# Attention scores as two products in 64x128 tiles a step, in place of four in 64x64 tiles

## The chip, the core and the metric

The kernel runs on one core of a Trainium2 chip. The metric is the device time of one execution in microseconds (us). The kernel before took 1121.53 us, the median of three runs (1121.16 to 1121.66).

## The reference

All values are 32-bit floats. The input `x` has 8 batches of 512 rows of 256 columns. Four blocks follow one another, each with a layernorm in front and its result added to `x`: a linear attention without scores, a feed-forward block, a softmax attention with 16 heads of 64 columns, and the same feed-forward block again. The change is in the third block:

```python
q = jnp.einsum('bsd,hpd->bhsp', x, q_w) + q_b
k = jnp.einsum('bsd,hpd->bhsp', x, k_w) + k_b
v = jnp.einsum('bsd,hpd->bhsp', x, v_w) + v_b
scores = jnp.einsum('bhqp,bhkp->bhqk', q, k) / jnp.sqrt(jnp.float32(P))
attn = jax.nn.softmax(scores, axis=2)          # over the queries
ctx = jnp.einsum('bhqk,bhkp->bqhp', attn, v)
concat = ctx.reshape(ctx.shape[0], ctx.shape[1], H * P)
out = concat @ l_w.T + l_b
```

The softmax runs over the queries, so that each key has a maximum and a sum of its own. The kernel therefore keeps keys on partitions and queries along the row, and it divides the rows of `v`, not the scores, by the sums.

## The kernel before

**Heads go in pairs.** Eight batches of eight pairs make 64 pairs, numbered `g`. A pair's transposed queries and keys lie in one buffer `qk`: partitions 0 to 63 hold the first head's 64 columns, partitions 64 to 127 the second's. A pair has four steps `c`, one for each block of 128 keys. In the notes below a step is one pair and one block of keys.

**A step of scores** (`scores`, line 1308) takes a pair of PSUM banks, `ps[0]` for the first head and `ps[1]` for the second; there are three such pairs of banks, taken in turn. Each bank gets 128 keys by 512 queries. TensorE fills them with four products (line 1320): two halves of 64 keys by two heads. Each has 64 contraction rows (a head's columns) and 64 weight columns (half of the keys), and so takes a quarter of the 128x128 array. The four use the four quarters. VectorE then takes the negated maximum of each row into `nm` (line 1326). `exps` (line 1331) has ScalarE write `e`, the exponentials, with their row sums (line 1337), which frees the banks.

**A step of contexts** (`context`, line 1361) multiplies `e` by the scaled values `vs` (line 1374). It too has four products in 64x64 tiles: two halves of the keys are now the contraction rows, and two heads of 64 columns are the weight columns. The two halves go to two further banks, `cx[0]` and `cx[1]`, and add up there over the four steps of a pair. At the end ScalarE copies one bank (line 1381) and VectorE adds the other (line 1382). `scale_v` (line 1345) makes `vs` on GpSimd from the sums' reciprocals.

**The order within attention** is written out in `attend` (line 1387). Attention runs in stages of two pairs, or of four pairs once in each batch. In a stage's first pair each step of scores is followed by a step of contexts of the pair before. In the other pairs the contexts lag one step and the last two stand together. TensorE's order for a stage of two pairs, with s for a step of scores and c for a step of contexts, is

```
s c s c s c s c | s s c s c s c c
```

and each further pair of a four-pair stage repeats the right half. Nothing else of TensorE stands between the steps of a stage, except in the first two pairs, whose contexts do not follow the pattern yet.

**Between the stages** TensorE does everything else in products of the whole 128x128 array: projections of queries, keys and values for the pairs to come (lines 999 and 1036), the output projection (line 1186), the linear attention (line 728 and others) and the two feed-forward blocks. A planner (`Order`) writes the order down when the program is built: chains of steps with estimated costs and due times are interleaved by the engines' estimated free times. It charges a step of scores and a step of contexts 0.86 us of TensorE each, and it charges 0.1 us (`CHANGE`, line 30) at either end of a stage. All of it is fixed before the program runs; at run time each engine works its own list in order and waits on semaphores.

**Two passes for one product.** A product of 32-bit floats appears in the profile as two weight loads and two matmuls, one after the other. The 2048 matmuls of line 1320 are thus 1024 products: 64 pairs, four steps, four products.

Of the kernel before, what the change touches and what calls it, by code (L numbers as in the profile page):

```python
# [14 lines left out]
P = 128  # L15
B, S, D = 8, 512, 256
H, HD = 16, 64
# [260 lines left out]
def kernel(ctx: ExitStack, tc: tile.TileContext, a: dict, out: bass.AP):  # L278
# [13 lines left out]
    nc = tc.nc  # L292
# [71 lines left out]
    def psum_tile(i, name):  # L364
        return psum.tile([P, 512], F32, tag=f"ps{i}", name=name)
# [942 lines left out]
    def scores(g, c):  # L1308

        qt, kt = qk[g][:, 0, :], qk[g][:, 1, :]  # L1310
        h = c // 2
        if c % 2 == 0:
            sums[g, h] = small.tile([P, 2, 2], F32, tag="sums", name=f"sums_{g}_{h}")
        i, since = order.take_pair()
        ps = [psum_tile(2 * i + j, f"sc_{g}_{c}_{j}") for j in range(2)]
        for m in range(2):
            keys = slice(c * P + m * HD, c * P + (m + 1) * HD)
            for j in range(2):
                hs = slice(j * HD, (j + 1) * HD)
                nc.tensor.matmul(  # L1320
                    ps[j][m * HD : (m + 1) * HD, :], lhsT=kt[hs, keys], rhs=qt[hs, :],
                    start=True, stop=True,
                )
        nm = small.tile([P, 2], F32, tag="nm", name=f"nm_{g}_{c}")
        for j in range(2):
            nc.vector.tensor_reduce(nm[:, j : j + 1], ps[j], AX.X, ALU.max, negate=True)  # L1326
        ready = order.place("T", 0.86, max(since, order.marks[f"qk_{g - g % 2}"]))
        scored[g, c] = i, ps, nm, order.place("V", 1.2, ready)
        order.keep_pair(i, 1e9)
# [57 lines left out]
    def attend(first, n):  # L1387

        for g in range(first, first + n):
            behind = 1 if g > first else 0  # L1390
            for c in range(NT):
                if c == 3 and g < first + n - 1:
                    order.at_once(scale_v(g, 0))
                scores(g, c)
                if c == 1 and g > first:
                    order.at_once(scale_v(g - 1, 1))
                if g > 0 and c >= behind:
                    context(g - 1, c - behind)
                elif g == 0:
                    order.fill(BANK)  # L1400
                if behind and c == 3:
                    context(g - 1, 3)
                exps(g, c)
                order.fill(0.0, 1.0)
# [116 lines left out]
```

## Time and profile before

| | value |
| --- | --- |
| time, median of 3 runs | 1121.53 us |
| time of the profiled execution | 1121.81 us |
| its span, first to last instruction | 1119.7 us |
| TensorE matmuls (PE) | 1105.3 us busy, 99%, 6938 instructions |
| TensorE weight loads (PEld) | 743.6 us busy, 66%, 6938 instructions |
| VectorE (DVE) | 798.4 us, 71% |
| ScalarE (ACT) | 678.3 us, 61% |
| GpSimd (POOL) | 590.0 us, 53% |
| DMA engines, mean | 31 GB/s |
| granted TensorE clock | 1.000 |

The profile is of one execution, and its times are in microseconds from the start of the span. The time of the profiled execution is 2.1 us longer than the span. A row of a group names line, engine, operation, what is written and read, and the shape; then the number of instructions, the time in which at least one of them ran, the mean of one in nanoseconds, and the idle time of the engine before them. `64*64` or `128*128` ahead of a matmul's shape are the rows and columns of the array that it uses. Matmuls are pipelined and overlap, so that the distance between two starts says more than the duration of one. In a timeline the columns are start, length and the merged instructions of one group.

### The profile page before, as it was taken

Reading aid. Unit: us, or ns where it says so; the run is one execution under the profiler, and the core shown is the slowest. Engines: PE = TensorE matmul, PEld = TensorE weight load, DVE = VectorE, ACT = ScalarE, POOL = GpSimd, SP = SyncE. Lnnn points to the kernel's source line nnn. Section 1 sums busy time; section 2 is a strip of 40 time slices with the busy share of each in tenths; the row PEclk is TensorE's granted clock in tenths of the full one; section 3 lists DMA queues with packets and bytes.
Section 4 is the critical chain, followed back from the end, with each engine's and each line's share of the span. In section 5 each row is a group of like instructions: output and inputs, shape, how many; then the busy total and the mean of one; then the engine's idle time right before and its main releaser. Section 6 shows DMA issues by size and latency. Waiting matters only on the chain.

```text
span 1119.7 us, 19677 instructions
## 1 busy us (share of the span) xinstructions
PE 1105.3 (99%) x6938; PEld 743.6 (66%) x6938; DVE 798.4 (71%) x1749; ACT 678.3 (61%) x1779; POOL 590.0 (53%) x909
## 2 busy tenths in 40 slices
PE   7999999999999999999999999999999999999998
PEld 4655646676766777667767667677675766756557
DVE  5778587768677685776857687667786668766765
ACT  4665586359456584566836767556676467554663
POOL 3596425462565735757356563575644865254321
PEclk9999999999999999999999999999999999999999
DMA  8001001120112201111011120211101121001101
GB/s 296 15 11 30 10 2 20 20 39 1 20 38 39 39 1 21 53 22 38 11 29 38 20 38 2 57 20 20 38 11 29 20 39 20 1 20 34 19 2 38
DMA packets 83874, 34.18 MB, mean 31 GB/s; under 512 B 73152, under 2 KB 82496, under 8 KB 83264
## 3 DMA queue, kind: packets, MB, share of 16 engines
q1 hardware_dynamic: 82736, 31.74, 12.6%
q8 instruction: 55, 0.90, 0.3%
q10 hardware_dynamic: 1008, 1.18, 0.3%
q14 instruction: 43, 0.35, 0.1%
q0 software_dynamic: 32, 0.00, 0.0%
HBM read 10.89 MB, written 4.19 MB: 13 GB/s over the span
## 4 chain that ended last, share of the span: by engine, by line
PE 96%; DVE 2%; ACT 0%; issue 0%; POOL 0%; DMA 0%; DVEq 0%; ACTq 0%
PE sc L1320 20%; PE cx L1374 20%; PE m_qk L999 17%; PE m_v L1036 8%; PE m_y L1186 8%; PE kv L728 5%; PE o_g L473 2%; PE r_g L473 2%; PE o_f L473 2%; PE q L473 2%; PE k_f L585 2%; PE r_f L473 2%; PE m_k_g L646 2%; PE y L473 1%; PE v L1075 1%; PE qk L1292 1%
## 5 line engine op out<-in xcount | busy, mean ns | idle before, releaser
L1337 ACT ACTIVATE e<-sc,nm 128x512 f32<-128x512 f32 x512 | 346.2, 693 | 99.8 <-DVE nm L1326 98.4
L1326 DVE TENSOR_REDUCE nm<-sc 128x1 f32<-128x512 f32 x512 | 321.6, 681 | 21.9 <-PE sc L1320 20.6
L1320 PE MATMUL sc<-qk 64*64 64x512 f32 x2048 | 284.7, 593 | 0.2
L1374 PE MATMUL cx<-e,vs 64*64 64x512 f32 x2048 | 283.5, 590 | 0.0
L1354 POOL TENSOR_TENSOR vs<-v,rs 128x256 f32<-128x256 f32 x128 | 78.5, 614 | 256.9 <-DVE rs L1350 247.8
L1374 PEld LDWEIGHTS cx<-e,vs 64*64 64x64 f32 x2048 | 107.5, 133 | 115.8 <-issue 77.5
L1320 PEld LDWEIGHTS sc<-qk 64*64 64x64 f32 x2048 | 105.9, 132 | 112.8 <-issue 67.4
L1337 ACT ACTIVATION_READ_ACCUMULATOR e<-sc,nm 128x1 f32 x512 | 107.2, 209 | 0.0
L1007 ACT ACTIVATE qk<-m_qk,bias 128x256 f32<-128x256 f32 x124 | 52.0, 473 | 64.8 <-PE m_qk L999 64.3
L1382 DVE TENSOR_TENSOR ctx<-cx,ctx 128x512 f32<-128x512 f32 x64 | 44.3, 692 | 44.2 <-ACT ctx L1381 44.2
L1015 DVE SCALAR_TENSOR_TENSOR qk<-m_qk,dbias,qk 128x256 f32<-128x256 f32 x124 | 53.9, 478 | 21.3 <-PE m_qk L999 20.4
L1381 ACT COPY ctx<-cx 128x512 f32<-128x512 f32 x64 | 37.8, 590 | 33.5 <-PE cx L1374 33.0
L728 PE MATMUL kv<-wkv,xrFalse 128*128 128x512 f32 x112 | 53.6, 606 | 0.0
L452 POOL COPY xrFalse<-xnFalse 128x512 uint16<-128x512 uint16 x72 | 42.1, 616 | 4.8 <-ACT xnFalse L425 4.8
L461 POOL COPY xrFalse<-xkFalse 128x1024 uint16<-128x1024 uint16 x24 | 32.1, 1338 | 21.3 <-DMA xkFalse<-xrFalse 21.2
L1186 PE MATMUL m_y<-ctx,al 128*128 128x256 f32 x168 | 40.1, 381 | 0.0
L999 PE MATMUL m_qk<-xta,aq 128*128 128x256 f32 x124 | 37.4, 383 | 0.0
L999 PE MATMUL m_qk<-xta,sums_q 128*128 128x256 f32 x124 | 37.2, 382 | 0.0
L999 PE MATMUL m_qk<-xts,aq 128*128 128x256 f32 x124 | 37.0, 380 | 0.1
L999 PE MATMUL m_qk<-xts,ak 128*128 128x256 f32 x124 | 36.9, 379 | 0.0
L999 PE MATMUL m_qk<-xta,sums_k 128*128 128x256 f32 x124 | 36.9, 379 | 0.0
L999 PE MATMUL m_qk<-xta,ak 128*128 128x256 f32 x124 | 36.9, 379 | 0.0
(281 smaller groups left out, 2123.9 us busy)
## 6 DMA issues: line engine op xcount, KB each, us to landing
out<-x SPq DMA_DIRECT2D x15, 256.0 KB, 2.1
x<-in_x SPq DMA_DIRECT2D x6, 512.0 KB, 4.0
aq<-in_aq SPq DMA_DIRECT2D x1, 1024.0 KB, 8.2
ak<-in_ak SPq DMA_DIRECT2D x1, 1024.0 KB, 10.2
av<-in_av SPq DMA_DIRECT2D x1, 1024.0 KB, 12.2
al<-in_al SPq DMA_DIRECT2D x1, 1024.0 KB, 5.2
xkFalse<-xrFalse SPq DMA_TRANSPOSE x36, 3.0
x<-in_x ACTq DMA_DIRECT2D x4, 128.0 KB, 4.0
```

What stands on the lines that cost most here:

```text
L473: nc.tensor.matmul(ps[:, u * D : (u + 1) * D], lhsT=lhs[i][:, u * P : (u + 1) * P], rhs=rhs[i], start=(i == 0), stop=(i == n - 1),)
L728: nc.tensor.matmul(ps, lhsT=xt[:, kc, u * P : (u + 1) * P], rhs=wkv[:, kc, :], start=(kc == 0), stop=(kc == KC - 1),)
L999: nc.tensor.matmul(ps[:, w * HS : (w + 1) * HS], lhsT=lhs[w][n - 1], rhs=block_of_rows(b, n), start=start and w == 0, stop=True, skip_grou ...
L1007: nc.scalar.activation(dst[:, w, :], ps[:, w, :], AF.Identity, bias=bias[:, w, p : p + 1])
L1015: nc.vector.scalar_tensor_tensor(dst[:, w, :], ps[:, w, :], dbias[:, w, p // 2 : p // 2 + 1], part[:, w, :], ALU.add, ALU.add,)
L1036: nc.tensor.matmul(ps[:, u * HS : (u + 1) * HS], lhsT=block_of_rows(b, n)[:, u * P : (u + 1) * P], rhs=rhs[n - 1], start=start and u == 0, ...
L1186: nc.tensor.matmul(ps, lhsT=lhs[n - 1][:, g, :], rhs=rhs[g][n - 1], start=first and g == 0, stop=True, skip_group_check=True,)
L1320: nc.tensor.matmul(ps[j][m * HD : (m + 1) * HD, :], lhsT=kt[hs, keys], rhs=qt[hs, :], start=True, stop=True,)
L1326: nc.vector.tensor_reduce(nm[:, j : j + 1], ps[j], AX.X, ALU.max, negate=True)
L1337: nc.scalar.activation(e[:, j, :], ps[j], AF.Exp, bias=nm[:, j : j + 1], accum_out=sums[g, h][:, c % 2, j : j + 1],)
L1354: nc.gpsimd.tensor_tensor(vs, vh[b, p // 4][:, 2 * h : 2 * h + 2, cols].rearrange("p t (j d) -> p t j d", j=2), rs.unsqueeze(3).to_broadca ...
L1374: nc.tensor.matmul(cx[m][j * HD : (j + 1) * HD, :], lhsT=vsc[g, c // 2][ks, c % 2, j, :], rhs=es[g, c][ks, j, :], start=(c == 0), stop=(c ...
```

## The change

One product now covers all 128 keys of a block, so that a step of scores has two products in place of four, one for each head. Each has 64 contraction rows and 128 weight columns: half of the array's rows and all of its columns. Both write a bank of their own, as before. Contexts stay in 64x64 tiles. The maxima, the exponentials and the planner's estimates are not touched.

```diff
         ps = [psum_tile(2 * i + j, f"sc_{g}_{c}_{j}") for j in range(2)]
-        for m in range(2):
-            keys = slice(c * P + m * HD, c * P + (m + 1) * HD)
-            for j in range(2):
-                hs = slice(j * HD, (j + 1) * HD)
-                nc.tensor.matmul(
-                    ps[j][m * HD : (m + 1) * HD, :], lhsT=kt[hs, keys], rhs=qt[hs, :],
-                    start=True, stop=True,
-                )
+        for j in range(2):
+            hs = slice(j * HD, (j + 1) * HD)
+            nc.tensor.matmul(
+                ps[j], lhsT=kt[hs, c * P : (c + 1) * P], rhs=qt[hs, :], start=True, stop=True
+            )
         nm = small.tile([P, 2], F32, tag="nm", name=f"nm_{g}_{c}")
```

## The prediction

> **What bounds the kernel now.** I read the page first: engines, granted clock, chain of waits, costliest groups. The chain that ended last is TensorE for 96% of the span, and the two attention groups hold the most of it.
>
> ```profile
> PE 1105.3 (99%) x6938; PEld 743.6 (66%) x6938; DVE 798.4 (71%) x1749; ACT 678.3 (61%) x1779; POOL 590.0 (53%) x909
> ...
> PEclk9999999999999999999999999999999999999999
> ...
> PE 96%; DVE 2%; ACT 0%; issue 0%; POOL 0%; DMA 0%; DVEq 0%; ACTq 0%
> ...
> L1337 ACT ACTIVATE e<-sc,nm 128x512 f32<-128x512 f32 x512 | 346.2, 693 | 99.8 <-DVE nm L1326 98.4
> ...
> L1320 PE MATMUL sc<-qk 64*64 64x512 f32 x2048 | 284.7, 593 | 0.2
> L1374 PE MATMUL cx<-e,vs 64*64 64x512 f32 x2048 | 283.5, 590 | 0.0
> ...
> L1337 ACT ACTIVATION_READ_ACCUMULATOR e<-sc,nm 128x1 f32 x512 | 107.2, 209 | 0.0
> ```
>
> TensorE is never short of work and its clock is full, so whatever it gains or loses goes straight into the time. Next I read TensorE's timeline through one stage of two pairs, with the work on either side of it.
>
> ```profile
> 621.17 1.03 PE L1036 MATMUL m_v<-sums_v,xta 128*128 128x256 f32 x4
> 622.12 1.09 PE L1320 MATMUL sc<-qk 64*64 64x512 f32 x8
> 623.03 1.04 PE L1374 MATMUL cx<-e,vs 64*64 64x512 f32 x8
> 623.89 1.04 PE L1320 MATMUL sc<-qk 64*64 64x512 f32 x8
> ...
> 634.19 1.90 PE L1374 MATMUL cx<-e,vs 64*64 64x512 f32 x16
> 636.02 3.72 PE L585 MATMUL k_f<-xkFalse,fk 128*128 128x256 f32 x16
> 639.58 1.24 PE L473 MATMUL r_f<-fr,xrFalse 128*128 128x256 f32 x5
> ```
>
> Inside the stage a step of scores or contexts starts 0.86 us after the one before (623.03 to 623.89): eight passes in four tiles, so two rounds of 0.429. A pass of 256 columns in the whole array takes half of that, 0.2156. So the pace is the number of streamed columns, whatever the tile, and the four tiles of a round run side by side: single starts lie 7 ns apart.
>
> The changes of tile are dearer. **Into 64x64:** four passes from 621.17 end their turn at 622.03, but the scores start at 622.12, 0.09 late; and their first step lasts 0.91, not 0.86, another 0.05. **Out to 128x128:** two steps from 634.19 end their turn at 635.91, the fourth tile's 0.02 later, and the next product starts at 636.02, 0.09 late; its 16 passes take 3.56 in place of 3.45, another 0.105. Start by start, all 26 changes in and all 26 out agree: 0.093 to 0.095, then 0.051; 0.090 or 0.091, then 0.105.
>
> The weight loads' timeline, at the stage that begins at 583.48, tells the two parts apart.
>
> ```profile
> 582.74 0.41 PEld L473 LDWEIGHTS o_g<-fv,xnTrue 128*128 128x128 f32 x2
> 583.48 0.21 PEld L1320 LDWEIGHTS sc<-qk 64*64 64x64 f32 x8 [0.33 <-issue]
> 583.96 0.15 PEld L1374 LDWEIGHTS cx<-e,vs 64*64 64x64 f32 x4 [0.28 <-issue]
> 584.39 0.15 PEld L1374 LDWEIGHTS cx<-e,vs 64*64 64x64 f32 x4 [0.28 <-issue]
> ```
>
> Within one kind of tile the loads run a round ahead of their matmuls: loads for the contexts start at 583.96, the contexts at 584.39. At the change the first load starts only as the first matmul does, 583.48. So about 0.09 us is an emptying of the array, and the 0.05 (64 columns) or 0.105 (128 columns) behind it is a load that nothing hides.
>
> **The change part by part.** *Removed:* 512 products, so 1024 of 6938 matmuls and as many loads. This saves no stream time. A step is still two rounds of 512 columns, 2 x 0.429, because the four quarter tiles were already side by side, and the two halves will be if the two heads' row halves still overlap. Nothing in the trace shows 64x128; the bounds are 0.86 a step (halves overlap, as the two row halves of the 64x64 round do) and 1.72 (they don't). I take 0.86, which is the row with the same two row halves. Issue does not limit a pass (7 ns between starts), so fewer passes give nothing back.
>
> *Added:* changes of tile shape inside the stages. In the instruction order of the changed kernel TensorE's list is otherwise the same; it holds 212 places where contexts follow scores, 188 where scores follow contexts, and 25 entries from whole-array work into scores. Today all these steps are 64x64, and the first two kinds cost nothing.
>
> The price of a change between 64x64 and 64x128 is not in the trace. Below it is zero (a stop of the array can't win time of itself); the nearest rows are the 52 changes above, and I take them: the array empties (0.09), then loads for as many columns as the new tile has. Contexts after scores: 212 x (0.094 + 0.051) = 30.7 us. Scores after contexts: 188 x (0.090 + 0.105) = 36.7 us. Entries: the first load is 128 wide, not 64, 25 x 0.054 = 1.4 us. Together 68.8 us.
>
> The load of a 64x128 tile has half the rows of the 128x128 one; were it priced as a 64-column load, the sum falls by 188 x 0.054 = 10 us. Did the array empty twice as fast because only 64 rows are in use, it falls by 400 x 0.046 = 18 us.
>
> The Trainium skill (TensorEngine Tiling, Key Properties) says that changing the tiling mode, not merely the tile, drains TensorE, and lists 64x128 and 64x64 as different modes. The 52 rows show it only between 128x128 and 64x64.
>
> *Given back:* a stage of two pairs lasts 13.89 us from its first scores to the next whole-array product in 10 of 15 cases, one of four pairs 27.63 in two of 8; the others are longer, by 1.8 us in all for the short ones, 4.0 for the long ones, and the stage at 65.19 by 0.8. That is 6.6 us of waits inside stages. ScalarE makes them: two exponentials of 0.693 + 0.209 are 1.80 a step, and TensorE's two steps 1.72. After the change TensorE takes 1.72 + 0.145 + 0.195 = 2.06, ScalarE no longer lags, and I let all 6.6 go. It is closest in the later pairs of a long stage, with three changes each way: TensorE 8 x 0.859 + 3 x 0.34 = 7.89 a pair, ScalarE 4 x 1.80 and a copy of 0.59 (line 1381), 7.81. Nothing new is late: VectorE's two maxima are 1.36 a step (0.681 each), contexts lag the scores by a whole pair less a step, and the DMA, GpSimd and filler lists are not moved. Keeping all these waits is the upper end, +6.6.
>
> *Sum:* span 1119.7 + 68.8 - 6.6 = 1181.9; with the 2.1 us that the profiled execution (1121.81) has around its span 1184.0. The median before is 0.3 lower than that execution, so I say 1184. The case's own range is 1166 (empties twice as fast) to 1191 (no wait absorbed).
>
> **The rivals.** *Loads not hidden at all in half-array tiles.* If the scores' second pass had to wait for its load as the first does, add 256 x 0.105 = 27 us: 1211. For it: two half-array tiles in a round leave no column of their rows idle to load into. The Trainium skill (TensorE: Matmul & The Clock Gate, part 3) has a rule to that effect: a weight load overlaps a running matmul only where its row group differs; by it the sum would be 1211. Against it: whole-array loads of 0.19 us, with no other row group left, lie wholly under passes 0.2156 apart.
>
> *Not slower: a change of width alone does not stop the array.* The mechanism is that TensorE tracks quarters, a 64x128 tile being two of them, and goes on loading ahead. In the trace the change is always of rows and columns at once, so it can't say which of them stops the array; the four tiles also run at offsets of up to 0.3 us from one another where ScalarE is late. Then only the entries' 1.4 us is left: 1123, within 0.2% of before. This decides below 6.6 / 400 = 0.016 us a change, where the waits given back pay for the changes. Against it stand 52 of 52 changes at 0.145 or 0.195.
>
> *Half of the price:* only the load is exposed (212 x 0.051 + 188 x 0.105 + 1.4 - 6.6 = 25) or only the emptying (400 x 0.092 - 6.6 = 30): 1147 to 1152.
>
> *The two halves don't overlap:* 256 steps x 0.859 = 220 us more, 1404. Against it, the row halves of 64x64 rounds start 7 ns apart, into the same pairs of banks.
>
> **How the numbers follow.** Forecast 0.74; unhidden loads 0.08; no stop 0.08; half price 0.06; no overlap 0.04. The range from 1165 to 1212 takes in the first two, 0.82. A difference of 0.2% (2.2 us) is about the least that can be told from none: the no-stop case gives 0.05 to "same", 0.02 to "faster" (some waits go too) and 0.01 to "slower"; the others are all slower.
>
> **What would show it.** PE should have 5914 matmuls, 1024 of them scores on 64*128. Stages of two pairs (7 changes one way, 6 the other) should last 13.89 + 7 x 0.145 + 6 x 0.195 + 0.05 = 16.1 us, those of four pairs (13 and 12) 31.9, and the work between them should be as long as before. In the timeline, contexts should start about 0.95 after a step of scores' start and take 0.91 to their end of turn, and no load should run ahead across a change. Loads ahead of a change and stages of 13.9 would make the prediction wrong on the low side, scores 1.7 us apart in the double steps on the high side.

## The result, and the profile after

The changed kernel takes 1189.4 us, the median of four runs (1188.1 to 1189.8), against 1121.5 before. The ratio is 1.060, with a 95% interval of 1.0588 to 1.0612: 68 us slower, 5 us above the forecast. The profiled execution has a span of 1187.0 us, 67.3 more than before.

The lines of the page that answer to those of before:

```profile
PE 1172.8 (99%) x5914; PEld 672.5 (57%) x5914; DVE 803.8 (68%) x1749; ACT 683.8 (58%) x1779; POOL 588.4 (50%) x909
...
PEclk9999999999999999999999999999999999999999
...
L1318 PE MATMUL sc<-qk 64*128 64x512 f32 x1024 | 278.3, 633 | 0.2 <-DVE prev_f L493 0.2
L1371 PE MATMUL cx<-e,vs 64*64 64x512 f32 x2048 | 268.9, 610 | 0.0
```

TensorE has 1024 passes fewer, and its busy time rises by 67.5 us, as much as the span (67.3). The two attention rows do not show it: their union got shorter (284.7 to 278.3, 283.5 to 268.9), because scores and contexts no longer overlap. Whoever adds up rows would read a gain here. The starts have to be read, in TensorE's timeline through one stage of two pairs:

```profile
655.83 1.03 PE L1036 MATMUL m_v<-sums_v,xta 128*128 128x256 f32 x4
656.78 1.13 PE L1318 MATMUL sc<-qk 64*128 64x512 f32 x4
657.84 1.09 PE L1371 MATMUL cx<-e,vs 64*64 64x512 f32 x8
658.86 1.13 PE L1318 MATMUL sc<-qk 64*128 64x512 f32 x4
659.92 1.09 PE L1371 MATMUL cx<-e,vs 64*64 64x512 f32 x8
...
665.10 1.99 PE L1318 MATMUL sc<-qk 64*128 64x512 f32 x8
667.01 1.09 PE L1371 MATMUL cx<-e,vs 64*64 64x512 f32 x8
...
671.17 1.95 PE L1371 MATMUL cx<-e,vs 64*64 64x512 f32 x16
673.05 3.72 PE L585 MATMUL k_f<-xkFalse,fk 128*128 128x256 f32 x16
```

A step of scores now holds TensorE for 1.06 us (656.78 to 657.84), a step of contexts for 1.02, where both held it for 0.86. Two steps of scores in a row (665.10 to 667.01) take 1.91, so the second costs 0.85 (start by start 0.859): the wide products keep their pace, the change costs. The weight loads' timeline over the same stretch shows the second half of the price:

```profile
656.78 0.30 PEld L1318 LDWEIGHTS sc<-qk 64*128 64x128 f32 x4 [0.33 <-DVE prev_f L496]
657.84 0.21 PEld L1371 LDWEIGHTS cx<-e,vs 64*64 64x64 f32 x8 [0.76 <-issue]
658.86 0.30 PEld L1318 LDWEIGHTS sc<-qk 64*128 64x128 f32 x4 [0.81 <-DVE v L971]
659.92 0.21 PEld L1371 LDWEIGHTS cx<-e,vs 64*64 64x64 f32 x8 [0.76 <-issue]
```

The loads begin exactly when the matmuls of their step do; before, they ran a round ahead. The names of engines behind the arrows are releasers long done; that these distances of 1.06 and 1.02 return in nearly every stage (14 of the 15 of two pairs are equally long to about a hundredth) says that no semaphore sets them.

Measured from start to start over the whole trace, the changes cost what the table says. A round is one pass in every tile of the array. "Array empties" is the time from the last tile's start in the round ahead of the change to the first start behind it, less the length of a pass (0.429 us for 512 columns, 0.2156 for 256). "First load shows" is the time from the first to the second round behind the change, less a pass. The trace shows these two gaps and where the loads start; that the first of them is the array running empty is the reading that fits them.

| change | number | array empties, median | first load shows, median | tiles start apart by |
| --- | --- | --- | --- | --- |
| scores to contexts (64x128 to 64x64) | 212 | 0.090 | 0.051 | 0.007 |
| contexts to scores (64x64 to 64x128) | 188 | 0.090 | 0.104 | 0.020 |
| whole array to scores | 25 | 0.094 | 0.104 | 0 |
| contexts to whole array | 25 | 0.090 | 0.105 | 0.020 |

The last column is the time from the first to the last tile's start in the round ahead of the change: the gap before the next step counts from the last tile. Stages of two pairs last 16.26 or 16.27 us in 14 of 15 cases (16.50 in the other), those of four pairs 32.17 in all eight. The stages grew by 67.3 us in sum, and the stretches ahead of, between and behind them by 0.1 in sum.

### The profile page after: what moved, and what is told of

It is laid out like the page before. It is cut to its first block, busy times and chain, and to the rows that moved or that the text cites. A ratio compares the mean times of both kernels' runs of the same rounds, so it can differ in the third digit from the quotient of the medians.

```text
span 1187.0 us, 17543 instructions
## 1 busy us (share of the span) xinstructions
PE 1172.8 (99%) x5914; PEld 672.5 (57%) x5914; DVE 803.8 (68%) x1749; ACT 683.8 (58%) x1779; POOL 588.4 (50%) x909
## 5 line engine op out<-in xcount | busy, mean ns | idle before, releaser
L1318 PE MATMUL sc<-qk 64*128 64x512 f32 x1024 | 278.3, 633 | 0.2 <-DVE prev_f L493 0.2
L1371 PE MATMUL cx<-e,vs 64*64 64x512 f32 x2048 | 268.9, 610 | 0.0
L1318 PEld LDWEIGHTS sc<-qk 64*128 64x128 f32 x1024 | 81.6, 185 | 182.3 <-ACT e L1334 104.9
L1371 PEld LDWEIGHTS cx<-e,vs 64*64 64x64 f32 x2048 | 57.4, 131 | 184.8 <-issue 169.6
L1334 ACT ACTIVATION_READ_ACCUMULATOR e<-sc,nm 128x1 f32 x512 | 103.9, 203 | 0.0
L1015 DVE SCALAR_TENSOR_TENSOR qk<-m_qk,dbias,qk 128x256 f32<-128x256 f32 x124 | 53.9, 478 | 21.3 <-PE m_qk L999 20.5
```

The source lines that it names most:

```text
L1015: nc.vector.scalar_tensor_tensor(dst[:, w, :], ps[:, w, :], dbias[:, w, p // 2 : p // 2 + 1], part[:, w, :], ALU.add, ALU.add,)
L1318: nc.tensor.matmul(ps[j], lhsT=kt[hs, c * P : (c + 1) * P], rhs=qt[hs, :], start=True, stop=True)
L1334: nc.scalar.activation(e[:, j, :], ps[j], AF.Exp, bias=nm[:, j : j + 1], accum_out=sums[g, h][:, c % 2, j : j + 1],)
L1371: nc.tensor.matmul(cx[m][j * HD : (j + 1) * HD, :], lhsT=vsc[g, c // 2][ks, c % 2, j, :], rhs=es[g, c][ks, j, :], start=(c == 0), stop=(c ...
```

## The experiments

The theory: every change of tile shape empties the array and bares the load of the first round; 400 such changes stand inside the stages now, and nothing else has got slower. The rivals: the wide products or their loads are dear in themselves, or waits on other engines are part of the price.

**No changes, all products wide.** Contexts too go into 64x128 tiles.

```diff
-            for j in range(2):
-                nc.tensor.matmul(
-                    cx[m][j * HD : (j + 1) * HD, :], lhsT=vsc[g, c // 2][ks, c % 2, j, :],
-                    rhs=es[g, c][ks, j, :], start=(c == 0), stop=(c == NT - 1),
-                )
+            nc.tensor.matmul(
+                cx[m], lhsT=vsc[g, c // 2][ks, c % 2].rearrange("p j d -> p (j d)"),
+                rhs=es[g, c][ks, m, :], start=(c == 0), stop=(c == NT - 1),
+            )
```

> Both kinds of product in 64x128 tiles, so that no change of tile shape is left inside a stage; the waits, the loads of 128 columns and the 256 wide steps of scores all stay. Left out: each half of the keys is weighted with one head's exponentials for both heads, so half of the contexts' products. Theory (each change empties the array and bares one load): the 400 changes and their 67 us go, the waits on ScalarE of before (6.6 us) come back, entries stay 0.054 dearer each: about 1122 to 1123 us, stages of two pairs 13.9 to 14.6 us. Rival (the wide products themselves are slow, or their loads are never hidden): the price stays or doubles with twice as many wide products, 1189 us or more.

Measured: 1124.4 us, ratio 1.0023 (1.0014 to 1.0033), 1.4 us above the upper end of what was expected. TensorE's timeline:

```profile
622.80 1.13 PE L1318 MATMUL sc<-qk 64*128 64x512 f32 x4
623.76 1.02 PE L1370 MATMUL cx<-e,vs 64*128 64x512 f32 x4
624.62 1.02 PE L1318 MATMUL sc<-qk 64*128 64x512 f32 x4
625.48 1.02 PE L1370 MATMUL cx<-e,vs 64*128 64x512 f32 x4
```

The step of 0.86 is back, with twice as many wide products as in the changed kernel. Stages last 13.93 to 14.60 and 27.67 to 28.39, each 0.04 to 0.05 above the same stage of before: the wider first load, less 0.013 for fewer tiles at the exit. That is 1.1 us in sum; the profiled execution has another 1.3 us outside the stages, whose cause stays open. The wide products cost nothing of themselves, and loads of 128 columns hide within a row half as within the whole array.

**Fewer changes, first try.** The order within a stage becomes s s c c throughout; done once on the changed kernel and once on the kernel before, as a control.

```diff
-                if g > 0 and c >= behind:
-                    context(g - 1, c - behind)
+                if g > 0 and c % 2 == 1:
+                    context(g - 1, c - 1)
+                    context(g - 1, c)
...
-                if behind and c == 3:
-                    context(g - 1, 3)
```

> The changed kernel with two steps of scores and then two of contexts throughout a stage: 126 + 102 changes of shape inside the stages, not 212 + 188; the same 256 wide steps. Theory: 86 changes to contexts at 0.0905 + 0.051 + 0.007 and 86 back at 0.0905 + 0.105 + 0.02 go, 31 us: 1158 us, up to 1165 if ScalarE's waits return, since TensorE then needs 1.90 us a step against ScalarE's 1.80 and a quarter of a copy. Rival (price of the wide products, not of the changes): 1189 us.

> The kernel before (all 64x64) with the same order as in the run before this one. It has no change of shape inside a stage in either order. Theory: within 0.5% of 1121.5 us, as the order only moves waits on ScalarE. Rival (what the grouped order gains comes from the order, with whatever it does to waits): about 30 us less here as well, 1090 us.

Measured: 1190.9 us for the changed kernel so grouped (ratio 1.0619, 1.0603 to 1.0635), and 1153.7 for the control (1.0283, 1.0266 to 1.0300). Taken alone the first would refute the theory; the control shows that something else was changed: without any change of shape in a stage it lost 32 us. The stretches ahead of, between and behind the stages hold 21 us of them (684.4 us in all, 685.8 in the other run, where the two kernels have 663.2 and 663.3). Moving the steps had moved the planner's calls, and it had written another order of the other work: 428 of the 2842 places in the order of whole-array matmuls hold another product, in both runs. TensorE waited more, and part of the loss is a lower clock. The control's page, and its timeline at the end of one such stretch:

```profile
PE 1117.1 (97%) x6938; PEld 724.6 (63%) x6938; DVE 797.1 (69%) x1749; ACT 684.1 (59%) x1779; POOL 589.7 (51%) x909
...
PEclk9999999999989998999999999999999999999999
```

```profile
441.02 1.06 PE L999 MATMUL m_qk<-xta,aq 128*128 128x256 f32 x2
441.88 1.06 PE L999 MATMUL m_qk<-xta,ak 128*128 128x256 f32 x2
...
444.05 0.59 PE L999 MATMUL m_qk<-xts,sums_q 128*128 128x256 f32 x2
444.48 0.59 PE L999 MATMUL m_qk<-xts,sums_k 128*128 128x256 f32 x2
```

The granted clock was 0.50 in four stretches of the control, 20.5 us together (310.5 to 313.9, 327.6 to 334.4, 430.0 to 433.4, 436.8 to 443.6), and in four of the other run, 23.9 us together. Two passes take 0.86 us there, 0.43 behind it. In the control each such stretch begins in a wait of TensorE of 1.9 to 4.0 us or at most 1.3 us behind one; one wait of 2.5 us, at 247.8, has no such stretch behind it. TensorE was busy for 17.6 of the 20.5 us, so the low clock cost about 9 of the 32 us (an estimate: half of that time); the idle time, span less busy time, is 20.8 us longer than in the kernel before. No other profile here has such a stretch between its 13th us and the end of TensorE's work. Undisturbed stages of two pairs did last the 15.18 us that the table's prices give for three changes fewer each way, but the totals decide nothing.

**Fewer changes, planner left alone.** The products alone move: `context` makes its calls to the planner where it did, and a new function issues the matmuls of two steps together.

```diff
...
+        for d in (c, c + 1) if early else (c - 1, c) if c % 2 else ():
+            contexts_of(g, d)
...
-                    context(g - 1, c - behind)
+                    context(g - 1, c - behind, behind == 1 and c - behind in (0, 2))
```

> The changed kernel with two steps of scores and then two of contexts, as in the grouped run before, but with the planner's calls left where they were, so that all other work keeps its place on every engine's list. 126 + 102 changes inside the stages, not 212 + 188. Theory: 86 x 0.1485 + 86 x 0.2155 = 31 us less than the changed kernel, 1158 us; up to 1165 if waits return, since a later pair takes TensorE 6.87 + 0.73 = 7.6 us against ScalarE's 7.8. Rival (the price is in the wide products): 1189 us.

> The kernel before with the same regrouping, planner's calls left in place. No change of shape inside a stage in either order. Theory: 1121 to 1124 us, as only waits move, and stages of 13.89 and 27.63 us at the least. Rival (regrouping gains by itself): 1090 us.

Measured: 1168.1 us (ratio 1.0413, 1.0396 to 1.0430) and 1128.8 us (1.0062, 1.0047 to 1.0077). The stretches ahead of, between and behind the stages are as in both kernels again (663.3 and 662.9 us in sum), and every engine's other work stands in the order of before. TensorE's timeline of the regrouped changed kernel:

```profile
99.46 1.99 PE L1318 MATMUL sc<-qk 64*128 64x512 f32 x8
101.38 1.95 PE L1365 MATMUL cx<-e,vs 64*64 64x512 f32 x16
103.26 1.99 PE L1318 MATMUL sc<-qk 64*128 64x512 f32 x8
105.17 1.95 PE L1365 MATMUL cx<-e,vs 64*64 64x512 f32 x16
```

Undisturbed stages last 15.18 and 30.36 us. Against the control's 13.89 and 27.63 that is 1.29 and 2.73, and the prices of the table give 4 x 0.148 + 3 x 0.215 + 0.04 = 1.28 and 8 x 0.148 + 7 x 0.215 + 0.04 = 2.73. Against the changed kernel, 172 changes fewer gave 21 us, not 31, because waits came back: the stages hold about 10 us above their undisturbed lengths here, and 13 in the control, which has no change to slow TensorE. So both times lie above the upper ends of what was expected (1165 and 1124), by waits that were put too low; the rival's 1189 and 1090 are out.

**Narrower tiles at the change.** Each contexts product is split into two of 32 columns.

```diff
-            for j in range(2):
+            for j in range(4):
                 nc.tensor.matmul(
-                    cx[m][j * HD : (j + 1) * HD, :], lhsT=vsc[g, c // 2][ks, c % 2, j, :],
-                    rhs=es[g, c][ks, j, :], start=(c == 0), stop=(c == NT - 1),
+                    cx[m][j * 32 : (j + 1) * 32, :],
+                    lhsT=vsc[g, c // 2][ks, c % 2, j // 2, j % 2 * 32 : (j % 2 + 1) * 32],
+                    rhs=es[g, c][ks, j // 2, :], start=(c == 0), stop=(c == NT - 1),
                 )
```

> The changed kernel with each contexts product split in two, in 64x32 tiles: eight side by side in a round. As many changes as in the changed kernel. Theory, with its three terms apart: emptying 0.0905 both ways as before; the bare load follows the columns, so about 0.025 into contexts (was 0.051) and 0.105 into scores as before; the offset of the tiles' starts, 7 ns each, is 0.05 out of contexts (was 0.02). The two moves cancel: 212 x -0.026 + 188 x 0.028 = 0, so 1189 us within 3. Rival (load time follows rows or the number of loads): 0.05 to 0.1 into contexts, 1194 to 1205 us. Rival (the offset does not count, the emptying starts at the first tile's end): 1184 us.

Measured: 1189.7 us, ratio 1.0606 (1.0590 to 1.0622), the changed kernel's time within a few tenths. TensorE's timeline has the same distances as the changed kernel with twice the passes in a step of contexts:

```profile
657.16 1.13 PE L1318 MATMUL sc<-qk 64*128 64x512 f32 x4
658.22 1.09 PE L1371 MATMUL cx<-e,vs 64*32 64x512 f32 x16
659.24 1.13 PE L1318 MATMUL sc<-qk 64*128 64x512 f32 x4
```

Start by start the terms separate as expected: emptying 0.090 both ways, the bare load 0.024 into contexts and 0.104 into scores, the eight tiles 0.047 apart. So the load goes by columns (0.024, 0.051, 0.104 for 32, 64, 128), the emptying by neither the columns nor the number of tiles, and the offset by the number of tiles. That 4096 context passes cost what 2048 did also shows that the number of passes is no cost here.

**The waits given back.** The row sums are left out of the exponentials, on the kernel before and on the changed one.

```diff
+            nc.vector.memset(sums[g, h], 512.0)
...
-                accum_out=sums[g, h][:, c % 2, j : j + 1],
```

> The kernel before without the row sums of the exponentials (they are left out and set to 512), which takes the 0.209 us behind each of the 512 exponentials off ScalarE. Theory of the 6.6 us given back (ScalarE's 1.80 us a step is what TensorE's 1.72 waited for inside stages): ScalarE falls to 1.39 a step, the waits go, and the kernel takes 1115 to 1116 us with 13.89 and 27.63 us for all stages. Rival (the waits come from banks or from GpSimd's scaled values): 1121 us, unchanged.

> The changed kernel with the row sums left out in the same way. Theory: the changes of shape had already slowed TensorE to more than ScalarE's pace, no wait is left to give back: 1189 us within 1. Rival (waits on ScalarE are part of the price): up to 7 us less, 1182 us.

Measured: 1119.8 us on the kernel before, ratio 0.9981 (0.9972 to 0.9990), and 1188.9 us on the changed one, ratio 1.0596 to the kernel before (1.0582 to 1.0611), where the changed kernel has 1.060. On the changed kernel the theory holds: no wait was left. On the kernel before the gain is 2, not 6; its stages became 2.65 us shorter in sum. The waits of the weight loads, first of the kernel before and then without the sums, point to why:

```profile
PEld sc L1320 <- ACT e L1337: 19.8, 75, 0.5
...
PEld cx L1374 <- POOL vs L1354: 12.8, 36, 0.7
```

```profile
PEld cx L1374 <- POOL vs L1354: 14.6, 43, 0.5
PEld sc L1321 <- ACT e L1338: 13.0, 50, 0.5
```

The columns are the time in all, the number and the longest. Most of these are not TensorE's own waits, since a load may start late under a running pass; but the part behind ScalarE falls and the part behind GpSimd's scaled values does not. So 2.65 of the 6.6 us went with the row sums. Not all of that need be ScalarE's pace, since without the sums `vs` no longer has to wait for the exponentials either. For the rest the releasers name GpSimd's `vs` most often, which no run here tests by itself.

## Why the prediction was right, and where it was off

**The forecast's mechanism held.** The 400 new changes empty the array and bare a load, with the durations read from the 52 changes of before: in the median 0.090 and 0.051 or 0.104, and all but two of them within 0.003 of that (at those two a step of scores came 0.009 and 0.23 later). With none of them, the same wide products run at the old pace (1124.4 us). The Trainium skill's statement that a change of tiling mode drains TensorE (in TensorEngine Tiling (Array Packing), Key Properties) agrees with the trace, here for a change of columns alone (400 cases) and of rows alone (25 entries from the whole array).

**The term that was mis-sized is the price of a change.** The prediction saw the 0.02 between the four tiles' starts when it read the exit from a stage, and left it out where it priced the change. With 188 x 0.020 + 212 x 0.007 it is 5.2 us: 68.8 becomes 74.0, less 6.6 is 67.4, and the stages grew by 67.3. That is the miss of 5 us. (The 0.094 taken for the 212 measured 0.090, which is 0.8 us the other way; one change in the first stages, at 69.7 us, with its tiles 0.53 apart, takes back most of that.) The stage lengths of the forecast lack the same term: 16.1 and 31.9 us were named, 16.27 and 32.17 measured. In the kernel before, the offset costs nothing inside an undisturbed stage: steps follow at 0.859 although their tiles start 0.020 apart. Behind an emptying the next step counts from the last tile.

**Given back:** the size was right, the cause only in part. All but about 0.2 of the 6.6 us went, but they were not shown to be ScalarE's alone: without the row sums ScalarE needs less time a step than TensorE, and 4 us of waits were still there. To that extent the right size was luck.

**The bounds not needed:** loads of 128 columns show 0.104 with half of the rows too, so columns were the right row to go by, and the emptying is not shorter for 64 rows.

**The rivals.** Loads that never hide (1211) fell: the second step of a double lasts 0.86. The Trainium skill's rule behind it (TensorE: Matmul & The Clock Gate, part 3: a load overlaps a running matmul only in another row group) does not hold as worded in the double steps and in the all-wide run, where both row groups always hold a running pass and steps still follow at 0.859; the measurement decides. The no-stop case, half the price and halves that don't overlap are out by the table and by the 0.86 a step.

**One check was stated wrongly:** contexts were to start about 0.95 us after the scores. It is 1.06, since the scores' own bare load lies in between. The sum had counted it; that sentence had not.

## What to carry to other kernels

Where TensorE sets the time, a product's shape has to be judged with its neighbours: a shape that halves the instructions can cost 0.15 to 0.21 us each time TensorE changes to it or back. Price it by the distance between starts at the changes that the trace already has, the offset of the tiles included, and count the changes in the instruction order. An experiment that reorders steps under a planner needs a control, or must leave the planner's calls in place.

## What was not expected of the hardware

The array empties in 0.090 us whichever of 64x32, 64x64 and 64x128 it leaves, and in 0.094 from 128x128. The tiles of a round start about 7 ns apart (eight tiles: 0.047), which is free until something waits for the last one. Twice as many passes in half as wide tiles take the same time, 16.26 us for a stage with 64x32 contexts as with 64x64.
